# A graph layer with scatter-add: the layer norm without TensorE steps, sorting moved into the loop, early z additions moved

## The chip, the core and the metric

The kernel runs on one core of a Trainium2 chip. The core has five engines that run their own instruction streams and wait for each other through semaphores: TensorE (PE; weight loads are listed as PEld), VectorE (DVE), ScalarE (ACT), GpSimd (POOL) and SyncE (SP). DMAs are issued from the queues of SP, ACT and POOL. Matmul results lie in PSUM, all else on the chip in SBUF. The metric is the device time of one execution in microseconds (us); lower is better.

## The reference

6250 nodes with 64 features, 206,250 edges sorted by their target `dst`:

```python
h = jnp.maximum(_layernorm(x, axis=-1), 0.0)
msg = jax.nn.relu(h[src] + edge_attr)
agg = jax.ops.segment_sum(msg, dst, num_segments=N)
z = h + agg
out = x + jax.nn.relu(z @ W1 + b1) @ W2 + b2
```

For each edge a normalized row is fetched by its source, the edge's own row is added, and the result is summed into the row of its target. A small two-layer network follows.

## The kernel before

Edges come in 268 groups of 768 (128 partitions x 6 columns) and a short last one. The normalized rows are needed in three forms: `h_rows` in DRAM for gathers (POOL's indirect DMAs, one column of 128 rows each, `gather`, L204), `hp` in SBUF as three bf16 parts for fetching rows by TensorE, and `z`, features on partitions and nodes along the free axis, as the start of the sum.

*Two ways to fetch a row.* Half of the columns of a group come by gathers, the other half (a "unit" of three columns) by TensorE. For that the sources of each unit are sorted: `places` works out row and part of each source, the rank steps (`rank_at`, `rank_count`, `rank_of`, `rank_marks`, `rank_holds`, `rank_turn`, `source`) count within each part and write index lists to DRAM for a chunk of six units, 46 chunks in all; `find` and `back` turn these lists into one-hot matrices, and `slots_of` (L500) and `pick` (L516) multiply with them. Between the two, `slots_out` copies PSUM to `picked`.

*The sum.* `messages` makes the messages, `one_hot` the matrix of targets within a window of 32 nodes, `window_sum` (L615) multiplies the two, and `sum_into_z` (L578) adds the window to z at a place read at run time. `hidden`, `result` and `store` do the network for 512 nodes at a time when their rows are complete.

*Order.* The order on each engine is the order of the program's text (a manual schedule), so an instruction that waits holds up all behind it on its engine. The text runs as follows.

1. Loads; constants; `places(0, 2)` (chunks 0 and 1), `rank_at(0)`, `rank_count(0)`.
2. The layer norm in four quarters of 13 and 12 rows per partition (`CUTS`, L797): `ln_head` (sum, mean, subtraction on VectorE, square on ScalarE), `ln_rows` (sum of squares, root on ScalarE, reciprocal, scaling with the ReLU; then the write to `h_rows`), `ln_turn` (transposes on TensorE into one of three PSUM banks, four rows each, and their copies to z on ScalarE). The rank steps of chunk 0 are interleaved.
3. `slots_of_edges` (target of each edge within its group; a matmul spreads each group's base over the partitions), the loads and gathers of groups up to 6 (`enter`), `places(2, NCH)` for all other chunks, and `banks_begin` (four matmuls that prime the two pick banks).
4. The F0 loop (L829) over the first five groups, which are fetched by gathers alone. The first three gather raw rows of x, so that they need not wait for `h_rows`, and are normalized here (`norm_edges`). Into their gaps `fill` puts steps of `ln_parts`, which make hp. The rank steps of chunks 1 and 2 and the zeroing of the tail half of each `ea` buffer (`tails_begin`) lie here too, and one window sum and z addition per step.
5. The first slots and picks, and then 276 times `half(u)`: the loop over units. Each issues at most one group's loads and gathers nine groups ahead; the gathers wait for TensorE ("beats").

PSUM: one bank `rows` shared by all small products, three `half` banks for slots (the window sums have a corner of the first), two pick tiles of two banks each.

The four lines that set the second chunk of work in the layer norm:

```python
        if len(rows) > 1:
            ln_turn(*rows[-2])
        if r == CUTS[1]:
            rank_turn(0)
```

Of the kernel before, what the change touches and what calls it, by code (L numbers as in the profile page):

```python
# [75 lines left out]
BIAS, STEP = 4096, 512  # L76
CHECKS = [NG // 4, NG // 2, 3 * NG // 4, NG - 12]
# [4 lines left out]
def kernel(  # L82
# [80 lines left out]
    nc.vector.tensor_copy(ident_b, ident)  # L163
    ones_b = const.tile([P, P], F16, name="ones_b")
# [19 lines left out]
    nc.scalar.copy(z[D:], zero[D:].to_broadcast([P - D, N + W]))  # L184
# [53 lines left out]
    code = const.tile([P, NCH, CC], F32, name="code")  # L238
    assert PARTS <= S

    def from0_all(n):
        return from0[:, :n].unsqueeze(1).to_broadcast([P, RG, n, H])
# [12 lines left out]
    def places(c0, c1):  # L255
        n = c1 - c0
        row = lnp.tile([P, n, CC], I16, name="row", bufs=1)
        off = lnp.tile([P, n, CC], F32, name="off", bufs=1)
        second = lnp.tile([P, n, CC], I16, name="second", bufs=1)
        third = lnp.tile([P, n, CC], F32, name="third", bufs=1)  # L260
        own = lnp.tile([P, n, CC], F32, name="own", bufs=1)
        m, parts = stretches(src_sb, c0, c1)
        for src, w, gs in parts:
            nc.vector.tensor_copy(own.rearrange("p c s -> p (c s)")
                                  .rearrange("p (e w g j) -> p e w g j", w=2, g=m, j=H)[:, :, w, gs], src)
        nc.vector.tensor_scalar(row, own, 1.0 / RR, 0.5 / RR + 0.5, op0=ALU.mult, op1=ALU.add)
        nc.vector.scalar_tensor_tensor(off, row, float(-RR), own, op0=ALU.mult, op1=ALU.add)
        nc.vector.tensor_scalar(second, off, 1.0 / PARTS, (RR + 0.5) / PARTS - 0.5, op0=ALU.mult, op1=ALU.add)
        nc.vector.scalar_tensor_tensor(node[:, c0:c1], second, float(PP), row, op0=ALU.mult, op1=ALU.add)
        nc.vector.tensor_scalar(third, second, float(BB), quarter[:, 0:1], op0=ALU.is_equal, op1=ALU.mult)  # L270
        nc.vector.scalar_tensor_tensor(off, second, float(-PARTS), off, op0=ALU.mult, op1=ALU.add)
        nc.vector.scalar_tensor_tensor(part[:, c0:c1], off, float(RR), third, op0=ALU.add, op1=ALU.add)
        nc.vector.tensor_scalar(code[:, c0:c1], part[:, c0:c1], float(STEP), float(BIAS), op0=ALU.mult, op1=ALU.add)

    spot_rows = dram.tile([NCH * CC, P], BF16, name="spot_rows")
    ats, counts, marks, holds, ranks, spot_i = {}, {}, {}, {}, {}, {}

    def rank_at(c):
        ats[c] = rank.tile([P, RG, PARTS, H], F16, name="at")
        nc.vector.tensor_tensor(ats[c], over(part[:, c], PARTS), from0_all(PARTS), ALU.is_equal)  # L280

    def rank_count(c):
        ps = psum.tile([P, RG, PARTS, H], F32, name="rows", bufs=1)
        at = ats[c]
        nc.tensor.matmul(ps, upper, at, start=True, stop=False)  # L285
        for d in range(1, H):
            last = nc.tensor.matmul(ps[:, :, :, d:], ones_b, at[:, :, :, :H - d], start=False, stop=(d == H - 1))  # L287
        if c < 3:
            beats.append(last)
        counts[c] = rank.tile([P, RG, PARTS, H], F16, name="before", bufs=1)  # L290
        nc.scalar.copy(counts[c], ps)

    def rank_of(c):
# [7 lines left out]
        nc.vector.tensor_tensor(spot_i[c], ranks[c], code[:, c], ALU.add)  # L301
# [9 lines left out]
    def rank_holds(c):  # L311
        holds[c] = rank.tile([P, RG, S, H], F16, name="holds")
        nc.vector.tensor_tensor(holds[c], over(ranks[c], S), from0_all(S), ALU.is_equal)  # L313
# [9 lines left out]
    def rank_turn(c):  # L323
        turned = psum.tile([CC, P], BF16, name="rows", bufs=1)
        nc.tensor.transpose(turned, spot_i.pop(c).bitcast(BF16), ident_b)  # L325
        sp = rank.tile([CC, P], BF16, name="sp")
# [5 lines left out]
    def source(c):  # L332
# [7 lines left out]
        if c < 2:  # L340
            beats.append(last)
        col = rank.tile([PARTS, RG * S], I16, name="source")
# [7 lines left out]
    halves_made = [0]  # L350

    def next_half():
        halves_made[0] += 1
        return half_banks[halves_made[0] % 3]
# [11 lines left out]
    def ln_rows(r, n, sq):  # L366
        h = x_rows(r, n)
        v = lnp.tile([PP, n], F32, name="ln_v")
        nc.vector.tensor_reduce(v, sq, AX.X, ALU.add)
        nc.scalar.activation(v, v, AF.Sqrt, bias=eps_sb[:PP], scale=1.0 / D)  # L370
        nc.vector.reciprocal(v, v)
# [7 lines left out]

    def ln_turn(r, m, h):  # L380
        zv = z[:D, :NP].rearrange("d (p r) -> d p r", r=RR)
        for i in range(0, m, 4):
            n = min(4, m - i)
            pt = next_half()[:D].rearrange("d (u p) -> d u p", u=4)
            for u in range(n):
                nc.tensor.transpose(pt[:, u, :], h[:, i + u, :], ident[:PP, :PP])  # L386
            nc.scalar.copy(zv[:, :, r + i:r + i + n], pt[:, :n].rearrange("d u p -> d p u"))
# [11 lines left out]
    def combine(xg, ea, n):  # L399
        nc.vector.tensor_tensor(xg[:, :n], xg[:, :n], ea[:, :n], ALU.add)  # L400
        msg = work.tile([P, G, D], F32, name="msg", bufs=3)
# [144 lines left out]
    def norm_edges(xg):  # L546
# [4 lines left out]
        sq = work.tile([P, G, D], F32, name="msg", bufs=3)  # L551
# [11 lines left out]
    pick_banks = [psum.tile([P, H + 1, 4, D], F32, name=f"pick{i}", bufs=1) for i in range(2)]  # L563
# [16 lines left out]
    def one_hot(u):  # L580
        g, (lo, hi) = group_of(u), span(u)
        n = hi - lo
        oh = work.tile([P, G, W], F32, name="oh")
# [9 lines left out]
    def messages(u):  # L593
# [10 lines left out]
        msg = work.tile([P, G, D], F32, name="msg", bufs=3)  # L604
# [91 lines left out]
    def half(u):  # L696
# [60 lines left out]
        chunk(u + 13, rank_count)  # L757
        chunk(u + 12, rank_of)
        chunk(u + 11, rank_marks)
        chunk(u + 11, rank_turn)  # L760
        chunk(u + 10, rank_holds)
        chunk(u + 10, rank_fits)
        chunk(u + 9, source)
        if g in CHECKS and is_first(u):
# [13 lines left out]
    def slots_of_edges():  # L778
# [3 lines left out]
        nc.tensor.matmul(pb[:, :NG + 1], ones[0:1, :], base, start=True, stop=True)  # L782
        nc.vector.scalar_tensor_tensor(
# [8 lines left out]

    heads, rows = [], []
    places(0, 2)
    rank_at(0)
    rank_count(0)
    for r, to in zip(CUTS, CUTS[1:]):  # L797
        heads.append(ln_head(r, to - r))
        if r == 0:
            rank_of(0)  # L800
            rank_marks(0)
            rank_holds(0)
        if len(heads) > 1:
            rows.append(ln_rows(*heads[-2]))
        if len(rows) > 1:
            ln_turn(*rows[-2])
        if r == CUTS[1]:
            rank_turn(0)
            source(0)
    rows.append(ln_rows(*heads[-1]))  # L810
    ln_turn(*rows[-2])
# [7 lines left out]
    slots_of_edges()  # L819
    ln_turn(*rows[-1])  # L820
# [3 lines left out]
    places(2, NCH)  # L824
# [3 lines left out]
    banks_begin()  # L828
    for g in range(F0):  # L829
        for i in range(g * LOOK // F0, (g + 1) * LOOK // F0):  # L830
            tails_begin(i)
# [6 lines left out]
        if g == 1:  # L838
            rank_of(1)
            rank_marks(1)  # L840
            rank_turn(1)
        if g == 2:
            rank_holds(1)
            rank_fits(1)
            source(1)
        if g == 3:
            rank_at(2)
# [7 lines left out]
    sum_into_z(-LAG - 1)  # L855
    while split:
        fill()
    ln_stack.close()
# [16 lines left out]
    for b in range(BB + 1):  # L875
        find(1, b)
    back_far(1)
# [89 lines left out]
```

## Time and profile before

| | us |
|---|---|
| median of 3 runs | 1443.79 |
| lowest, highest | 1442.95, 1453.53 |
| the profiled execution | 1449.7 |
| its span, first to last instruction | 1447.9 |

Busy shares of that span: TensorE 79%, VectorE 67%, ScalarE 66%, GpSimd 56%. The mean granted clock of TensorE was 0.974.

In the views, each line of a timeline gives start and duration in us, engine, line of the code (L...), operation, what is written <- what is read, shapes, count, and in brackets how long the engine had been idle and what released it ("remote" and "another core or an unknown queue" are releases whose origin the profile doesn't have; with one core they are semaphores within it). Groups give busy time, mean ns of one, and the idle time ahead of them. "issue" is waiting that the profile doesn't explain.

### The profile page before, as it was taken

What the parts mean: (1) busy time and instruction counts of PE and PEld (TensorE: products, weight loads), DVE (VectorE), ACT (ScalarE), POOL (GpSimd) and SP (SyncE); (2) the same over time, 40 slices, a digit from 0 to 9 for tenths busy, and PEclk for the clock granted to TensorE, in tenths of its full rate; (3) what the DMA queues carried; (4) which work ended last, traced back from release to release, by engine and by line L of the source; (5) the groups of instructions that cost most, each with busy time, mean ns of one, the idle gap of its engine ahead of it and who ended that gap; (6) DMA issues with size and microseconds to landing.
All of it is one profiled execution on the core that took longest, in us unless ns stands there. A gap on an engine that the chain in (4) does not pass through costs nothing.

```text
span 1447.9 us, 55550 instructions
## 1 busy us (share of the span) xinstructions
PE 1142.2 (79%) x23305; PEld 899.5 (62%) x23305; DVE 977.1 (67%) x2686; ACT 956.8 (66%) x1979; POOL 806.7 (56%) x798
## 2 busy tenths in 40 slices
PE   3158888888788788888888888888888788888887
PEld 2046666666666666666666666666666666666666
DVE  7656666666667677666676667667666666766666
ACT  5356666667667676676676667667666666666666
POOL 5755546565555655555655565555565655556450
PEclk9579999999999999999999999999999999999999
DMA  5333534445444443444444443444444443435341
GB/s 169 90 108 108 150 99 114 130 118 139 109 118 116 139 125 106 124 118 139 109 119 121 129 124 112 124 106 144 116 116 120 134 123 108 134 107 141 114 111 35
DMA packets 115259, 172.40 MB, mean 119 GB/s; under 512 B 28603, under 2 KB 83772, under 8 KB 115004
## 3 DMA queue, kind: packets, MB, share of 16 engines
q1 hardware_dynamic: 89912, 143.05, 32.8%
q0 software_dynamic: 25088, 25.74, 9.1%
q8 instruction: 185, 3.03, 0.9%
q14 instruction: 70, 0.57, 0.1%
q10 hardware_dynamic: 4, 0.01, 0.0%
HBM read 164.86 MB, written 3.84 MB: 117 GB/s over the span
## 4 chain that ended last, share of the span: by engine, by line
PE 77%; issue 17%; DVE 2%; another core or an unknown queue 1%; ACT 1%; POOL 1%; DMA 1%; DVEq 0%; ACTq 0%; POOLq 0%
PE half L500 33%; PE pick L516 31%; PE half L615 9%; PE rows L339 1%; PE rows L287 1%; PE rows L652 1%; POOL xr L204 1%; PE rows L642 1%; PE rows L285 1%; PE rows L325 0%; ACT z L184 0%; DVE hp L397 0%; PE half L386 0%; DVE found L468 0%
## 5 line engine op out<-in xcount | busy, mean ns | idle before, releaser
L204 POOL DMA_INDIRECT xg<-h_rows,src_sb x754 | 772.6, 1025 | 585.0 <-PE half L500 448.5
L500 PE MATMUL half<-hp,found 128*32 128x192 bf16 x14352 | 498.8, 249 | 238.7 <-issue 219.7
L509 ACT CAST picked<-half 128x384 bf16<-128x384 f32 x828 | 369.7, 481 | 395.8 <-remote 222.0
L500 PEld LDWEIGHTS <-found 128*32 128x32 bf16 x14352 | 317.9, 96 | 367.6 <-issue 342.0
L516 PE MATMUL pick<-picked,backs 128*128 128x192 bf16 x4968 | 465.3, 248 | 3.9 <-issue 2.2
L516 PEld LDWEIGHTS <-backs 128*128 128x128 bf16 x4968 | 401.1, 99 | 51.7 <-issue 49.6
L578 DVE TENSOR_TENSOR z<-z,half 128x32 f32 x281 | 52.7, 187 | 380.8 <-issue 174.8
L487 DVE TENSOR_SCALAR backs<-spots,ids 128x768 bf16<-128x768 int16 x690 | 257.9, 416 | 7.5 <-issue 2.0
L603 DVE TENSOR_REDUCE ea<-pick 128x192 f32<-128x576 f32 x276 | 207.9, 753 | 47.9 <-PE pick L516 30.8
L468 DVE TENSOR_SCALAR found<-sources,nodes_of 128x1536 bf16<-128x1536 int16 (+1 forms) x414 | 203.8, 520 | 0.3 <-issue 0.2
L525 ACT COPY pick<-ea 128x576 f32<-128x576 f32 x264 | 168.9, 640 | 0.0
L615 PE MATMUL half<-oh,msg 128*64 128x32 f32 x3224 | 151.1, 227 | 2.7 <-DVE z L578 2.1
L605 ACT ACTIVATE msg<-ea 128x384 f32<-128x384 f32 (+2 forms) x281 | 146.6, 522 | 9.3 <-issue 4.1
L615 PEld LDWEIGHTS half<-oh,msg 128*64 128x64 f32 x3224 | 119.6, 138 | 46.0 <-issue 34.6
L477 ACT ACTIVATE dist<-spots,far 128x768 bf16<-128x768 int16 x138 | 129.9, 942 | 0.0
L480 ACT ACTIVATE backs<-dist,ones 128x768 bf16<-128x768 bf16 x138 | 129.5, 939 | 0.3 <-ACT dist L477 0.3
L584 DVE TENSOR_TENSOR oh<-slot,slots 128x192 f32<-128x192 int16 (+2 forms) x281 | 95.2, 339 | 8.0 <-remote 4.7
L600 DVE TENSOR_TENSOR ea<-ea,xg 128x192 f32<-128x192 f32 x252 | 88.3, 350 | 0.8 <-issue 0.4
L344 ACT CAST source<-rows 24x64 int16<-24x64 f32 x138 | 28.0, 203 | 21.0 <-PE rows L339 11.5
L339 PE MATMUL rows<-holds,marks 128*96 128x96 f16 x276 | 25.8, 231 | 12.7 <-DVE holds L313 8.7
L285 PE MATMUL rows<-at,upper 128*128 128x432 f16 x46 | 16.5, 358 | 21.8 <-issue 11.1
L339 PEld LDWEIGHTS <-marks 128*96 128x96 f16 x276 | 22.9, 147 | 12.9 <-DVE holds L313 8.8
(110 smaller groups left out, 431.1 us busy)
## 6 DMA issues: line engine op xcount, KB each, us to landing
sources<-source_row SPq DMA_DIRECT2D x138, 384.0 KB
ea<-in_edge_attr_dram SPq DMA_DIRECT2D x268, 192.0 KB
spots<-spot_rows SPq DMA_DIRECT2D x138, 192.0 KB
xg<-h_rows,src_sb POOLq DMA_INDIRECT x754
xb<-in_x_dram SPq DMA_DIRECT2D x12, 128.0 KB
out_dram<-o SPq DMA_DIRECT2D x12, 128.0 KB
h_rows<-x SPq DMA_DIRECT2D x3, 384.0 KB
dst_sb<-in_dst_main_dram SPq DMA_DIRECT2D x1, 804.0 KB
```

What stands on the lines that cost most here:

```text
L204: it = nc.gpsimd.indirect_dma_start(out=xg[:, j, :], out_offset=None, in_=rows[:, :], in_offset=bass.IndirectOffsetOnAxis(ap=idx[:, j:j + ...
L468: nc.vector.tensor_scalar(found[k][:, b * PARTS:b * PARTS + n].rearrange("p m i s -> p (m i s)"), sources[k][:, :n * 2 * S], nodes_of[:, b ...
L477: nc.scalar.activation(dists[k], spots[k].bitcast(I16), AF.Abs, bias=far)
L480: nc.scalar.activation(backs[k][:, Q - 1].rearrange("p t s -> p (t s)"), dists.pop(k), AF.Relu, bias=ones[:, 0:1], scale=-1.0)
L487: nc.vector.tensor_scalar(backs[k][:, q].rearrange("p t s -> p (t s)"), spots[k].bitcast(I16), ids[:, q:q + 1], None, op0=ALU.is_equal)
L500: last = nc.tensor.matmul(ps[j * S:(j + 1) * S, u], found[k][:, m, i, :], hp[:, min(m, RR - 1)].rearrange("p t d -> p (t d)"), start=(b == ...
L509: nc.scalar.copy(picked[k][:, n0:n0 + 2], halves.pop((k, n0)))
L516: last = nc.tensor.matmul(ps[:, u, :3].rearrange("p t d -> p (t d)"), backs[k][:, q, i * H + u, :], picked[k][:, i * Q + q], start=False, ...
L525: nc.scalar.copy(picks[u][:, :H, :3], parts)
L603: nc.vector.tensor_reduce(ea[:, c0:c0 + H], picks.pop(u)[:, :H, :3].rearrange("p j t d -> p j d t"), AX.X, ALU.add)
L605: nc.scalar.activation(msg[:, lo:hi], ea[:, lo:hi], AF.Relu)
L615: last = nc.tensor.matmul(pa[i * D:(i + 1) * D], msg[:, j, :], oh[:, j, :], start=(j < lo + 2), stop=(j >= hi - 2))
```

## The change

- **Layer norm.** `ln_rows` is split into `ln_var` (sum of squares and root) and the rest. Two heads are begun, then quarter by quarter. No rank step and no transpose is left in it. `rank_count(0)` and all that follows of chunk 0 come behind, then the zeroing of the lower half of z, which stood at the start on ScalarE; the twelve `tails_begin` stand at the start instead.
- **Transposes.** `ln_turn` only issues the transposes, into the pick banks (four turns of 512 columns), in the steps 0 to 3 of the F0 loop; the copies to z (`ln_turned`) come a step later, in steps 1 to 4. `banks_begin` comes behind the loop.
- **Sorting.** `places` works in 16-bit tiles borrowed from another buffer (`ow`) and gives way after each instruction. Chunks 0 and 1 are done at the start, 2 to 5 behind the layer norm, and the other 40 in three calls (6 to 21, 22 to 37, 38 to 45) in the main loop, one instruction per unit. `code` is gone; `part` holds an offset, and `from_b` is a second iota for it.
- **Handing back.** Each TensorE step with a reader on ScalarE is split in two (`rank_counted`, `rank_turned`, `sourced`), so that the reader can stand later in the text. In the main loop both halves stand next to each other as before.
- **z additions** of the first three groups move behind the first slots. `oh` has four buffers for two, `msg` four for three. `slots_of_edges` has its matmul in `bases`, with `places(2, 6)` between.

```diff
+PLACED = [0, 2, 6, 22, 38, NCH]
...
-    nc.scalar.copy(z[D:], zero[D:].to_broadcast([P - D, N + W]))
...
     def places(c0, c1):
         n = c1 - c0
+        held = [work.tile([P, WB], F32, name="ow").bitcast(I16) for _ in range(2)]
...
         nc.vector.tensor_scalar(row, own, 1.0 / RR, 0.5 / RR + 0.5, op0=ALU.mult, op1=ALU.add)
+        yield
...
-        nc.vector.tensor_scalar(code[:, c0:c1], part[:, c0:c1], float(STEP), float(BIAS), op0=ALU.mult, op1=ALU.add)
...
     pick_banks = [psum.tile([P, H + 1, 4, D], F32, name=f"pick{i}", bufs=1) for i in range(2)]
+    def next_turn():
+        i = turns_made[0] % 4
+        turns_made[0] += 1
+        return pick_banks[i // 2].rearrange("p j t d -> p (j t d)")[:, i % 2 * 512:][:, :512]
...
+    def ln_turned():
+        zv = z[:D, :NP].rearrange("d (p r) -> d p r", r=RR)
+        for pt, r, n in turned_rows:
+            nc.scalar.copy(zv[:, :, r:r + n], pt[:, :n].rearrange("d u p -> d p u"))
+        turned_rows.clear()
...
+        for c, to in zip(PLACED[2:], PLACED[3:]):
+            if u == max(0, 2 * RG * (c // 2) - 60):
+                searches.append(places(c, to))
         if g in CHECKS and is_first(u):
             searches.append(find_left(CHECKS.index(g)))
-        elif searches and next(searches[0], True):
+        if searches and next(searches[0], True):
             searches.pop(0)
...
+    for i in range(LOOK):
+        tails_begin(i)
+    for _ in places(0, 2):
+        pass
     rank_at(0)
+    quarters = list(zip(CUTS, CUTS[1:]))
+    heads = [ln_head(r, to - r) for r, to in quarters[:2]]
+    rows = []
+    for r, to in quarters[2:]:
+        v = ln_var(*heads.pop(0))
+        heads.append(ln_head(r, to - r))
+        rows.append(ln_rows(*v))
+    for v in [ln_var(*heads.pop(0)) for _ in range(2)]:
+        rows.append(ln_rows(*v))
     rank_count(0)
+    rank_counted(0)
+    nc.scalar.copy(z[D:], zero[D:].to_broadcast([P - D, N + W]))
+    rank_of(0)
+    rank_marks(0)
+    rank_turn(0)
+    rank_turned(0)
+    rank_holds(0)
+    source(0)
+    sourced(0)
+    pb = bases()
     split = [ln_parts(*r) for r in rows]
...
+    for _ in places(2, PLACED[2]):
+        pass
+    slots_of_edges(pb)
     rank_fits(0)
     for g in range(F0 + 2):
         enter(g)
-    places(2, NCH)
...
-    banks_begin()
     for g in range(F0):
...
         starts_for(g)
+        if g >= RAW:
+            fill()
...
+        ln_turned()
+        if g < len(rows):
+            ln_turn(*rows[g])
         if g >= 1:
             window_sum(g - 1 - F0)
-        if g > LAG:
-            sum_into_z(g - LAG - 1 - F0)
...
+    rank_counted(2)
+    banks_begin()
...
+    for g in range(F0 - LAG):
+        sum_into_z(g - F0)
     back_far(1)
```

More of the change, by code (lines that the diff above doesn't have):

```diff
@@ L256, in places, with at @@
         n = c1 - c0
[L257 to L261, printed above, removed]
+        held = [work.tile([P, WB], F32, name="ow").bitcast(I16) for _ in range(2)]
+        def at(i):
+            return held[i // 3][:, i % 3 * n * CC:][:, :n * CC].rearrange("p (c s) -> p c s", s=CC)
+        own, off, row, second, third = at(0), at(1), at(3), at(4), at(5).bitcast(F16)
         m, parts = stretches(src_sb, c0, c1)
```

95 lines of the change are left out of this document (49 added, 46 removed).

## The prediction

> **What bounds the kernel now.** I read the page first, then the stages, then the lead-in (everything ahead of the 276 half units) in the timeline. The page's chain line and two of its groups (busy, mean ns | idle before, releaser):
>
> ```profile
> span 1447.9 us, 55550 instructions
> PE 77%; issue 17%; DVE 2%; another core or an unknown queue 1%; ACT 1%; POOL 1%; DMA 1%; DVEq 0%; ACTq 0%; POOLq 0%
> L204 POOL DMA_INDIRECT xg<-h_rows,src_sb x754 | 772.6, 1025 | 585.0 <-PE half L500 448.5
> L578 DVE TENSOR_TENSOR z<-z,half 128x32 f32 x281 | 52.7, 187 | 380.8 <-issue 174.8
> ```
>
> TensorE holds the end for 77% of the span; VectorE and the gathers on POOL have room in the loop. The stages (busy time of PE, PEld, DVE, ACT, POOL, then granted clock, DMA share, GB/s):
>
> ```profile
> 60.00:80.00 20.00, 4.26 (x45) 3.04 (x45) 5.16 (x14) 6.21 (x14) 13.27 (x14) 0.50 0.28 73
> 300.00:600.00 300.00, 247.64 (x5095) 194.90 (x5093) 204.42 (x563) 202.52 (x423) 170.45 (x167) 0.99 0.44 121
> ```
>
> From 300 us on TensorE is busy 83% of the time. In the lead-in no engine is full: at 60 to 80 us TensorE works 4.3 of 20 us, at half the clock, and VectorE 5.2. So the lead-in is made of waits, and the change is nearly all there. Two places hold them. The first is the layer norm (start, duration, idle before and its releaser):
>
> ```profile
> 21.42 1.06 PE L386 MATMUL half<-ident,x 128*64 128x128 f32 x4 [1.10 <-ACT z L387]
> 24.30 1.08 ACT L387 COPY z<-half 64x512 f32<-64x512 f32 x2 [2.94 <-remote]
> 25.00 1.92 PE L386 MATMUL half<-ident,x 128*64 128x128 f32 x8 [2.52 <-ACT z L387]
> 29.25 1.70 ACT L387 COPY z<-half 64x512 f32<-64x512 f32 x3 [3.05 <-remote]
> 29.95 2.77 PE L386 MATMUL half<-ident,x 128*64 128x128 f32 x12 [3.03 <-ACT z L387]
> 31.05 0.65 ACT L387 COPY z<-half 64x512 f32<-64x512 f32 x1
> 31.43 0.96 DVE L372 SCALAR_TENSOR_TENSOR x<-x,ln_v 128x768 f32<-128x768 f32 x1
> 35.62 0.94 POOL L204 DMA_INDIRECT xr<-h_rows,src_sb  x1 [8.39 <-DMA h_rows<-x]
> ```
>
> Four transposes that begin at 29.95 are answered at 31.05, 1.1 us later. The four from 21.42 are answered at 24.30, 2.9 us later, and of the eight from 25.00 the first answer comes at 29.25: TensorE's answers come 1.8 and 3.1 us late. ScalarE stands at these copies, with the next square or root of the layer norm queued behind them, and VectorE stands behind ScalarE. So the last normalized row is made at 32.39, and the first gather from h_rows waits for it until 35.62. The second place is the loop over the F0 = 5 first groups; the chain of waits has there:
>
> ```profile
> 61.95 3.31 issue
> 67.06 4.72 another core or an unknown queue
> 72.52 3.74 another core or an unknown queue
> 77.40 4.69 another core or an unknown queue
> ```
>
> 16.5 us in all. The first of them, with who is asked and who waits:
>
> ```profile
> 56.93 0.86 PE L615 MATMUL half<-oh,msg 128*64 128x32 f32 x12
> 65.26 0.36 DVE L584 TENSOR_TENSOR oh<-slot,slots 128x192 f32<-128x192 int16 x1 [3.31 <-issue]
> ```
>
> The one-hot at 65.26 needs the buffer that the window sum of 56.93 reads (two buffers), so that sum is answered after 8.3 us; the other three waits stand behind later sums in the same way, at a one-hot or at a z addition. The cause of the lateness isn't in the trace. It falls together with gathers in flight: the transposes from 29.95 are prompt, and POOL was idle for the 8.39 us ahead of 35.62.
>
> **The change part by part.** *Layer norm.* The ranks of chunk 0, the transposes and their z copies leave it, and the 5.42 us zeroing of z moves behind it; twelve small zeroings of the ea tails take its place on ScalarE, off the path as the zeroing was. What is left is VectorE's own work, here for the 13-row quarter:
>
> ```profile
> 6.45 1.02 DVE L359 TENSOR_REDUCE ln_s<-x 128x13 f32<-128x832 f32 x1 [0.44 <-DMA x<-in_x_dram]
> 7.51 0.18 DVE L360 TENSOR_SCALAR ln_s<-ln_s 128x13 f32<-128x13 f32 x1
> 7.72 1.02 DVE L361 TENSOR_TENSOR x<-x,ln_s 128x832 f32<-128x832 f32 x1
> 13.18 1.01 DVE L369 TENSOR_REDUCE ln_v<-ln_sq 128x13 f32<-128x832 f32 x1
> 14.56 0.24 DVE L371 RECIPROCAL ln_v<-ln_v 128x13 f32<-128x13 f32 x1 [0.37 <-issue]
> 14.84 1.02 DVE L372 SCALAR_TENSOR_TENSOR x<-x,ln_v 128x832 f32<-128x832 f32 x1
> ```
>
> 4.49 us for 13 rows, so 16.9 for 49. With two heads begun ahead, the squares and roots on ScalarE lie beside VectorE's next quarter; 0.6 us for the turns that stay bare. From 6.45 that ends at 24.0 and not at 32.4. POOL's 18 raw gathers end at 27.2 (35.62 less 8.39), so the first gather from h_rows comes at about 27 and not at 35.62.
>
> *Between layer norm and the F0 loop.* Before:
>
> ```profile
> 9.13 0.38 DVE L295 TENSOR_TENSOR before<-before,at 128x432 f16<-128x432 f16 x1 [0.39 <-ACT before L291]
> 10.65 0.55 DVE L313 TENSOR_TENSOR holds<-rank_of,from 128x576 f16<-128x576 f16 x1
> 3.14 5.42 ACT L184 COPY z<-zero 64x6282 f32<-64x6282 f32 x1
> 14.44 0.24 ACT L327 COPY sp<-rows 18x128 bf16<-18x128 bf16 x1
> 15.40 0.63 ACT L344 CAST source<-rows 24x64 int16<-24x64 f32 x3 [0.73 <-issue]
> 33.01 1.23 PE L782 MATMUL rows<-base,ones 1*128 1x269 f32 x2 [0.29 <-DVE base L780]
> 34.28 1.83 DVE L783 SCALAR_TENSOR_TENSOR slot<-dst_sb,rows 128x1608 int16<-128x1608 int32 x1 [1.42 <-PE rows L782]
> 36.31 0.80 DVE L264 CAST own<-src_sb 128x396 f32<-128x396 int32 x3
> 42.85 0.57 DVE L273 TENSOR_SCALAR code<-part 128x792 f32<-128x792 f16 x1
> ```
>
> places for 44 chunks takes from 36.31 to 43.42, 7.1 us, all of it ahead of the first message; four chunks stay, as ten instructions of 0.2 (the rows of 7.51 and 14.56), 2 us. VectorE alone then needs 2.1 (the ranks' five instructions, 9.13 to 11.20), 0.6 for base (32.39 to 33.01), 2 for places and 2.1 for the slots (1.83 and three short ones), 24.0 + 6.8 = 30.8. But the zeroing of z, put behind the last root, some 2 us ahead of the last row, holds ScalarE until 27.4, and transposition, source lines and the bases follow each other through one PSUM tile: 1.6 us for the two copies with the matmul between (14.44 to 16.03), 1.2 for the bases, so the slots begin at 30.3 and end at 32.4, and the loop begins at about 33. Before, its first instruction stood at 43.34.
>
> *The F0 loop.* VectorE's first instruction in it, and what follows behind it:
>
> ```profile
> 43.34 0.54 DVE L548 TENSOR_REDUCE raw_s<-xr 128x6 f32<-128x384 f32 x1
> 36.73 1.50 PE L570 MATMUL pick<-marks,ones_b 128*128 128x512 f16 x4
> 86.93 4.71 PE L500 MATMUL half<-hp,found 128*32 128x192 bf16 x104 [9.45 <-DVE found L468]
> 93.06 1.65 PE L516 MATMUL pick<-picked,backs 128*128 128x192 bf16 x18 [1.43 <-ACT pick L525]
> ```
>
> The three steps with raw rows take from 43.34 to the first of the four waits at 61.95, 18.6 us, and keep that: 33 + 18.6 = 51.6. The z additions and the buffer wait of the one-hots go (four buffers each; additions behind the slots), so 61.95 to 82.1 goes but for what the moved transposes put there. The first two quarters lie beside VectorE's long steps. The third and fourth don't, since steps 3 and 4 are short: 2.77 of transposes and three copies of 0.65 each, 2 x 4.7 = 9.4, with the last parts of hp beside them. The four priming matmuls of the pick banks, 1.5, now wait for the last copy, since the transposes use those banks. Then slots to first pick, 6.1, as at 86.93 to 93.06: 51.6 + 9.4 + 1.5 + 6.1 = 68.6, 24.5 us ahead of 93.06.
>
> *Late answers* are the unknown. Four handoffs from TensorE stand bare: the bases (33.01 to 34.28, prompt, no gather then; now gathers run), the third and fourth quarter, and the fourth quarter's start, queued behind a window sum. Lower end 0 (nothing can come early), upper end 4.7 each, the window sums' usual wait. I take 2 each, between the transposes' own 1.8 and 3.1 and the prompt ones: 8 us. **Net 16.5 us.**
>
> *The main loop.* 40 chunks of places go there, one instruction per half unit, 30 in all; by 7.1 us for 44 chunks they are at least 6.5 us, and by fixed parts about 10. VectorE idles 380.8/281 = 1.36 us ahead of each z addition, which covers one instruction of 0.3; if that cover were gone it would cost 10 us. I take 0. The cheaper code, iota and buffer edits cost nothing that is on the path.
>
> One row speaks against putting places under gathers:
>
> ```profile
> 39.87 1.32 POOL L204 DMA_INDIRECT xr<-h_rows,src_sb  x1 [0.30 <-issue]
> ```
>
> It ran beside places; the gather at 35.62, ahead of it, took 0.94. The Trainium skill, SBUF — State Buffer, "SBUF: two separate sides", says that GpSimd can't write a gather's descriptors while VectorE runs an operation in a mode that takes the port they share. By that rule the trace agrees, and 30 gathers in the loop would grow by 0.4, 12 us on POOL. POOL stands 448.5 us waiting for TensorE in the loop, so it isn't on the path, and the sum keeps its value either way.
>
> **The rivals.** *Late answers eat most of it*: 4.7 for each bare handoff, and 1.2 each for two half-covered ones (the second quarter, a msg buffer; about 3.5 us of VectorE work over them), 21 us, so a gain of about 3: 1440. For it: all four window sums are late; against it: half of the transposes are prompt. *Slower*: the same place, with the lateness of 56.93 to 65.26, 8.3 us: 4 x 8.3 + 2 x 4.8 = 43 against 24.5, 18 us slower, 1462. It turns to a loss above 5.3 us each; only one of the six late answers seen is so late. *Gathers decide*: POOL begins only 9 us earlier, so if the first units had to wait for it the gain would be 9: 1435. Against it: groups are entered 9 ahead, and POOL waits for TensorE.
>
> **How the numbers follow.** The profiled execution took 1449.7 (span 1447.9), 0.4% over the median of 1443.79; the 16.5 us are lead-in and come off either: 1433.2 there, 1427 as a median. Chances: forecast 0.60 (gains of 11 to 24.5), late answers 0.24, gathers 0.08, slower 0.08. Range: from all of 24.5, 1419, to the late-answer case, 1442; about 2 in 10 stay outside. About 1%, 14.4 us, is what can be told from no change: gains above it are most of the forecast, 0.56; within, 0.37; slower 0.07.
>
> **What would show it.** Last h_rows write issued at 24 and not 32.4; first raw_s near 33; no wait over 1 us at one-hots or z additions; first pick between 67 and 78; half units of the same length after. Wrong if ScalarE stands 4 us or more at the z copies of the third and fourth quarter, if the bases come after 35, or if units with a places instruction are longer than their neighbours.

## The result, and the profile after

The change makes no difference. The median after is 1450.19 us (14 runs, 1446.62 to 1453.16), the median before 1450.67 (14 runs, 1442.95 to 1456.8); after over before is 1.0002, 95% interval 0.9984 to 1.002. The forecast was 1427. Some 7 us of that distance are the base it was taken from, a median of three runs, 1443.79; the rest is a gain of 16.5 us that isn't there.

In some sets of runs (taken on one chip, one after the other) a half unit of the loop takes about 5.0 us and the kernel before 1427 to 1451, as above, in others about 3.5 and 1055 to 1056, with the changed kernel always on the same side; these are called long and short runs here.

The timeline of the changed kernel in its lead-in:

```profile
22.43 0.96 DVE L400 SCALAR_TENSOR_TENSOR x<-x,ln_v 128x768 f32<-128x768 f32 x1
28.55 0.95 POOL L207 DMA_INDIRECT xr<-h_rows,src_sb  x1 [0.30 <-issue]
32.52 0.55 DVE L583 TENSOR_REDUCE raw_s<-xr 128x6 f32<-128x384 f32 x1
49.47 0.55 DVE L583 TENSOR_REDUCE raw_s<-xr 128x6 f32<-128x384 f32 x1
55.48 0.22 DVE L584 TENSOR_SCALAR raw_s<-raw_s 128x6 f32<-128x6 f32 x1 [5.46 <-remote]
61.78 0.91 ACT L421 COPY z<-pick 64x512 f32<-64x512 f32 x2 [10.11 <-remote]
63.04 0.55 DVE L590 TENSOR_REDUCE raw_v<-msg 128x6 f32<-128x384 f32 x1 [4.73 <-ACT msg L587]
64.87 0.95 POOL L207 DMA_INDIRECT xg<-h_rows,src_sb  x1 [7.17 <-PE half L649]
86.51 0.48 ACT L544 CAST picked<-half 128x384 bf16<-128x384 f32 x1 [3.94 <-remote]
87.58 3.04 PE L551 MATMUL pick<-picked,backs 128*128 128x192 bf16 x18 [7.71 <-issue]
```

The first three lines are near the forecast: the last normalized row ends at 23.39, the first gather from `h_rows` starts at 28.55, the F0 loop at 32.52. Then things stand still. The line at 55.48 is the plainest: VectorE takes the mean of a sum that it has made itself in the instruction ahead (49.47), no other engine has a part in it, and it starts 5.46 us late. ScalarE stands for 10.11 us ahead of its copies of z at 61.78, and POOL, whose next gather waits for a window sum, stands for 7.17. The first pick comes at 87.58, 5.5 us ahead of the 93.06 of before; without the stops it would be near 68.

The loop, in the groups of the page (busy, mean ns | idle before, releaser), and its stages:

```profile
L207 POOL DMA_INDIRECT xg<-h_rows,src_sb x754 | 776.8, 1030 | 588.2 <-PE half L535 446.4
L612 DVE TENSOR_TENSOR z<-z,half 128x32 f32 x281 | 52.9, 188 | 369.1 <-issue 177.9
```

```profile
60.00:85.00 25.00, 12.42 (x193) 9.25 (x194) 13.85 (x32) 15.75 (x32) 12.94 (x12) 1.00 0.37 111
300.00:600.00 300.00, 248.41 (x5114) 195.57 (x5102) 206.80 (x574) 202.94 (x425) 171.65 (x168) 0.99 0.42 121
```

Busy times in the groups and in the stage from 300 to 600 are those of before within 1.2%. One of the three groups of places instructions lies in that stage, and the half units 71 to 83, which hold it, average 4.92 us in both kernels. So the places in the loop cost nothing that shows here, and the loop is as long as it was.

Where the 5.5 us went is seen from the gathers. Their starts, out of the two traces:

| gather | before, us | after, us |
|---|---|---|
| 19th, first from `h_rows` | 35.6 | 28.6 |
| 81st | 138.4 | 135.0 |
| 401st | 715.0 | 711.2 |
| last, 784th | 1408.8 | 1408.0 |

From the 19th to the 81st, 62 gathers, they take 1.66 us each before and 1.72 after; in a half unit with three gathers, 5.04 us in both, 1.68. The lead-in and the loop look like one stream of gathers at one pace, and the changed kernel starts it 7.1 us earlier and gives up half of that by the 81st.

### The profile page after: what moved, and what is told of

It reads as the page before. It is cut to its first block, busy times and chain, and to the rows that moved or that the text cites. A ratio compares the mean times of both kernels' runs of the same rounds, so it can differ in the third digit from the quotient of the medians.

```text
span 1448.1 us, 55574 instructions
## 1 busy us (share of the span) xinstructions
PE 1144.0 (79%) x23305; PEld 901.4 (62%) x23305; DVE 977.9 (68%) x2714; ACT 955.8 (66%) x1979; POOL 810.8 (56%) x799
## 5 line engine op out<-in xcount | busy, mean ns | idle before, releaser
L207 POOL DMA_INDIRECT xg<-h_rows,src_sb x754 | 776.8, 1030 | 588.2 <-PE half L535 446.4
L535 PE MATMUL half<-hp,found 128*32 128x192 bf16 x14352 | 497.4, 248 | 225.2 <-issue 215.4
L339 PE MATMUL rows<-ident_b,spot_i 128*18 128x128 bf16 x46 | 10.4, 226 | 24.9 <-DVE rank_of L312 17.3
L312 DVE TENSOR_REDUCE rank_of<-before 128x18 f16<-128x432 f16 x46 | 27.7, 603 | 2.2 <-issue 0.7
```

The source lines that it names most:

```text
L207: it = nc.gpsimd.indirect_dma_start(out=xg[:, j, :], out_offset=None, in_=rows[:, :], in_offset=bass.IndirectOffsetOnAxis(ap=idx[:, j:j + ...
L535: last = nc.tensor.matmul(ps[j * S:(j + 1) * S, u], found[k][:, m, i, :], hp[:, min(m, RR - 1)].rearrange("p t d -> p (t d)"), start=(b == ...
```

## The experiments

Two theories stood against each other at first. G: gathers that POOL issues back to back hold up the signals (semaphore updates) of all engines. P: TensorE's answers are late by themselves. A third, B, blamed the bytes that are moved.

### Gathers taken away, paced; transposes left out (short runs)

*lead_plain*: in `load`, the 36 gathers from `h_rows` ahead of the loop become plain DMAs.

```diff
+        if RAW <= g < 14:
+            nc.sync.dma_start(out=xg[:, lo:hi], in_=h_rows[:(hi - lo) * P].rearrange("(j p) d -> p j d", p=P))
+            return ea, xg
         gather(xg[:, lo:], src_sb[:, g * G + lo:g * G + hi], hi - lo, x if g < RAW else h_rows, behind)
```

> The changed kernel with its 36 gathers from h_rows ahead of the loop of half units (groups 3 to 13) put as plain DMAs of the same rows per partition and the same bytes on SP's queue, one per group; it fetches fixed rows in place of those named by src. Theory G (gathers issued back to back by POOL hold up the signals of all engines): the long waits between 38 and 90 us go, the first pick starts at 68 to 73 us and not at 87.6, and the profiled time falls by 14 to 19 from 1449.9, to 1431 to 1436, with half units unchanged at 5.04 us. Rival P (TensorE's answers are late by themselves, at half clock and with fp32 transposes): waits and first pick stay, 85 to 90. Rival B (the bytes moved hold things up): the same, 85 to 90.

*lead_paced*: in `gather`, behind each of these 36.

```diff
+            if lead[0] and rows is not x:
+                nc.gpsimd.iota(pad, pattern=[[1, PAD]], base=0, channel_multiplier=0,
+                               allow_small_or_imprecise_dtypes=True)
```

> The changed kernel with an iota of about 0.5 us on POOL behind each gather from h_rows ahead of the loop, so that gathers start every 1.8 us and not every 1.25. Theory G, with a shared path that needs 1.4 to 1.6 us per gather: the path keeps up, waits over 3 us in the F0 loop go, first pick at 69 to 76 us. If the number of gathers counts and not their pace, the waits spread and the first pick stays at 83 to 90. Rival P: first pick 85 to 90. The whole time: 1435 to 1450 by theory G, since the gathers of the loop must still be made; 1450 by the rivals.

*no_turns*: in the F0 loop, with z zeroed whole.

```diff
-        ln_turned()
-        if g < len(rows):
-            ln_turn(*rows[g])
```

> The changed kernel without the 49 transposes of h and their 13 copies to z in the F0 loop; z is zeroed whole and so lacks h. Theory G: gathers still run from 28 to 58 us and other handoffs are late in the place of these, first pick at 78 to 88. Rival P: nothing of the lateness is left, first pick at 60 to 70.

*all_plain*: the edit of lead_plain with `if g >= RAW`.

> The changed kernel with all gathers from h_rows, 766, put as plain DMAs of the same bytes on SP's queue, one per group, with no pacing behind TensorE; it fetches fixed rows. Theory G: the loop's half units are set by gathers too; without them they take 3.3 to 3.6 us and not 5.04, and the whole takes 1000 to 1080 us. Rival P (TensorE is the bound at 83% busy): half units of at least 4.2, 1230 us or more. Rival B (bytes): half units of 5.0, 1430 to 1450.

All four were short runs, where the kernel before took 1056.16: lead_plain 1047.15, lead_paced 1067.19, no_turns 1060.73, all_plain 1052.41 (one run each), with first picks at 66.0, 65.4, 62.7 and 66.7. Nothing was late in any of them, so they tell nothing of G, P and B. One number stands out: lead_paced. Its groups on POOL:

```profile
L210 POOL DMA_INDIRECT xg<-h_rows,src_sb x754 | 774.0, 1026 | 226.3 <-issue 95.7 <-PE half L541 51.4 <-DMA xg<-h_rows,src_sb 28.7
L216 POOL IOTA pad<- 128x112 f32 x36 | 9.7, 268 | 0.3
```

The iotas took 0.27 us each, about half of what had been expected. The idle time, 226.3 us, is 0.30 for each of 754 gathers: POOL never stopped. And 9.7 us of iotas in the lead-in put the end of this one run off by 9.8 against the changed kernel's 1057.39 in the next set.

### The two kernels in short runs

> The changed kernel itself, on whatever chip this falls to, since the kernel before took 1056.2 us on the chip of lead_plain, no_turns and all_plain, and 1450.7 on that of the first measurements. Theory G, widened: how long a gather holds up the signals of the engines differs from chip to chip, and the change acts on what is left. Where gathers take 1.6 us each out of a half unit of 5.04, first pick at 87.6, about 1450 and no difference from before. Where they don't (half units near 3.5), no wait over 2 us in the F0 loop, first pick at 62 to 67, and then either faster by about 10 us (places in the loop are covered) or the same within 3 (half units with a places instruction are longer, since TensorE and VectorE are at 94% and 92%).

> The kernel before, for its trace on the same chip. Theory G: where half units are near 3.5 us, the four waits at window sums (16.5 us in the first trace) are gone and its first pick comes at 74 to 79 and not at 93. Rival P, lateness is TensorE's own: the waits are there on any chip, first pick at 90 to 95.

The changed kernel took 1057.39, the kernel before 1055.38: 1.0011, 0.999 to 1.0033. So no difference here either, but by another way. First picks and POOL, after_again first, before_again second:

```profile
28.33 0.95 POOL L207 DMA_INDIRECT xr<-h_rows,src_sb  x1 [0.30 <-issue]
32.30 0.55 DVE L583 TENSOR_REDUCE raw_s<-xr 128x6 f32<-128x384 f32 x1
46.18 0.54 DVE L583 TENSOR_REDUCE raw_s<-xr 128x6 f32<-128x384 f32 x1
46.76 0.21 DVE L584 TENSOR_SCALAR raw_s<-raw_s 128x6 f32<-128x6 f32 x1
66.45 1.65 PE L551 MATMUL pick<-picked,backs 128*128 128x192 bf16 x18 [1.21 <-ACT pick L560]
```

```profile
31.32 0.95 POOL L204 DMA_INDIRECT xr<-h_rows,src_sb  x1 [4.04 <-DMA w_sb<-in_w_dram]
74.27 1.65 PE L516 MATMUL pick<-picked,backs 128*128 128x192 bf16 x18 [1.12 <-ACT pick L525]
```

VectorE's mean at 46.76 follows its sum by 0.04 us, where it came 5.46 late in the long run. The first pick at 66.45 is the forecast's sum without its late answers, 68.6, within 2.2. Before, it stands at 74.27 and not at 93.06: the same program runs without the four waits of 16.5 us behind window sums, so they are no fixed cost of TensorE's steps. The changed kernel is 7.8 us ahead at the first pick and at nothing at the end. POOL's groups say why, again after_again first:

```profile
L207 POOL DMA_INDIRECT xg<-h_rows,src_sb x754 | 769.1, 1020 | 229.9 <-issue 93.9 <-PE half L535 54.3 <-DMA xg<-h_rows,src_sb 27.7
L207 POOL DMA_INDIRECT xr<-in_x_dram,src_sb x18 | 19.1, 1059 | 5.4 <-issue 5.4
L207 POOL DMA_INDIRECT xr<-h_rows,src_sb x12 | 12.0, 1002 | 3.7 <-issue 3.7
```

```profile
L204 POOL DMA_INDIRECT xg<-h_rows,src_sb x754 | 764.7, 1014 | 229.9 <-issue 93.9 <-PE half L500 45.8 <-DMA xg<-h_rows,src_sb 34.2
L204 POOL DMA_INDIRECT xr<-in_x_dram,src_sb x18 | 18.5, 1030 | 5.4 <-issue 5.4
L204 POOL DMA_INDIRECT xr<-h_rows,src_sb x12 | 14.1, 1174 | 7.4 <-DMA w_sb<-in_w_dram 4.0 <-issue 3.4
```

Busy and idle added to the first gather's start (3.8 and 3.6) give 1043.0 and 1043.6, and the last gathers end at 1042.6 and 1043.4. POOL issues gathers without a pause from the start to the end; in the changed kernel only the one pause of 4.0 us is gone, and its gathers are longer by 4.4 in all. Call this theory S: the stream of gathers sets the end, and what comes ahead of it counts only where it moves the stream. The rival L has it that lead-in and loop add up, and the loop got longer.

### S against L (short runs)

> The kernel of lead_plain once more, timed beside before_lead_plain on one chip. Where half units are near 3.5 us: theory S (the stream of gathers, which POOL issues back to back from 4 to 1042 us, sets the end, so that what comes ahead of it counts for nothing) gives 1045 to 1050, some 8 us less than before_lead_plain, since here POOL begins its stream at the first units. Where half units are 5.04 (the first chip): theory G gives a first pick at 66 to 72 and 1430 to 1440; rivals P and B 85 to 90 and 1450.

*before_lead_plain* is the edit of lead_plain in the kernel before.

> The kernel before with the same 36 gathers put as plain DMAs of fixed rows. Where half units are near 3.5 us: theory S gives a first pick at 74, as in before_again, and a time 6 to 10 us above lead_plain_3, 1053 to 1058: the lead-in that the change saves then shows. Rival L (the loop of the changed kernel is longer by what the lead-in gained, places included): the same time as lead_plain_3 within 3 us. On the first chip: theory G gives a first pick at 72 to 78 and not at 93, and 1430 to 1440.

*places_left_out*:

```diff
-        for c, to in zip(PLACED[2:], PLACED[3:]):
-            if u == max(0, 2 * RG * (c // 2) - 60):
-                searches.append(places(c, to))
...
+    for t in (part, node):
+        nc.vector.tensor_copy(t[:, PLACED[2]:], t[:, 5:6].to_broadcast([P, NCH - PLACED[2], CC]))
```

> The changed kernel without the 30 instructions of places in the loop: part and node of chunks 6 to 45 are copies of chunk 5 (two instructions ahead of the loop), so other rows are summed. Rival L: half units of the stretch are shorter, 8 to 10 us less than the changed kernel, 1047 to 1050 where half units are near 3.5. Theory S: gathers beside VectorE get a little shorter, at most 4 us less, 1053 to 1058. On the first chip both give 1445 to 1451.

lead_plain_3 took 1043.2 (0.9894 of the kernel before, 0.9867 to 0.992), a little under the expected range, before_lead_plain 1053.04 (0.9974, 0.9952 to 0.9997). With the stream beginning only at the first units, the saved lead-in is worth 9.8 us by the medians, as S has it and L not. The two recorded runs lie only 2.9 us apart (1048.34 and 1051.28). Their gathers, lead_plain_3 first:

```profile
L207 POOL DMA_INDIRECT xg<-h_rows,src_sb x730 | 743.6, 1019 | 260.0 <-PE half L538 88.0 <-issue 87.8 <-DMA xg<-h_rows,src_sb 29.0
```

```profile
L204 POOL DMA_INDIRECT xg<-h_rows,src_sb x730 | 737.9, 1011 | 269.3 <-PE half L503 98.8 <-issue 88.8 <-DMA xg<-h_rows,src_sb 24.4
```

The stream of lead_plain_3 has 9.3 us less idle time and 5.7 us more of gathers, and its last gather ends 2.7 earlier. That the end goes with the stream is seen here too; the 9.8 us are not seen in this pair. places_left_out took 1049.68 (0.9957, 0.9933 to 0.998), with its number inside what L expected. Its gathers:

```profile
L207 POOL DMA_INDIRECT xg<-h_rows,src_sb x754 | 761.0, 1009 | 229.9 <-issue 94.5 <-PE half L535 49.7 <-DMA xg<-h_rows,src_sb 28.0
```

They take 8.1 us less than in after_again, the whole 7.7 less (5.7 by the ratios to the kernel before, as the two are of different sets), and POOL still never pauses (3.8 us, busy 792.0 and idle 239.0 give 1034.8, the last gather ends at 1034.5). So the end goes with the stream, as S has it, but by more than the 4 us that S allowed. And it isn't shown how places lengthen the stream. In after_again 31 gathers run beside one of the 30 places instructions; they take 1054 ns on average, the other 723 take 1019, which makes 1.1 us in all (2.0 in after_third). Set against the same gathers of places_left_out, they hold 1.3 of the 8.1 us. The same loop also differs between runs by some 5 us, 774.0 in lead_paced and 769.1 in after_again. Nor are the half units with a places instruction longer, as L has it: those from 71 to 83 average 3.43 us in after_again, 3.39 in places_left_out.

### Two more (long runs)

*places_ahead* does all of `places(6, 46)` ahead of the F0 loop.

```diff
+    for c, to in zip(PLACED[2:], PLACED[3:]):
+        for _ in places(c, to):
+            pass
     for g in range(F0):
         messages(g - F0)
```

> The changed kernel with its places for chunks 6 to 45 all done ahead of the F0 loop, and none in the loop of half units. VectorE's 24 instructions there put the first pick off by 6 to 10 us, to 72 to 77 where half units are near 3.5. Theory S (POOL's unbroken stream of gathers sets the end): the first pick doesn't count, the stream starts and runs as in the changed kernel and its gathers are shorter without places beside them, so 1047 to 1052, 4 to 8 us under the kernel before. Rival L (lead-in and loop add up): 1055 to 1060. On the first chip (half units of 5.04), theory G: 1445 to 1452, no difference from before.

*more_whole*:

```diff
-HEAD, PERIOD = 2 * RG - 1, 4 * RG - 1
+HEAD, PERIOD = 2 * RG - 1, 2 * RG - 1
-WHOLE = [F0 + RG - 1] + list(range(F0 + HEAD + 2 * RG - 1, NG + 1, PERIOD))
+WHOLE = [F0 + RG - 1] + list(range(F0 + HEAD + RG - 1, NG + 1, PERIOD))
...
-        n, g0 = (HEAD, F0) if c0 == 0 else (PERIOD, F0 + HEAD + (c0 - 2) // 4 * PERIOD)
+        n, g0 = (HEAD, F0) if c0 == 0 else (PERIOD, F0 + HEAD + (c0 - 2) // 2 * PERIOD)
```

> The changed kernel with every eleventh group, and not every twenty-third, fetched wholly by TensorE: 288 half units for 276, 36 gathers fewer. Where half units are near 3.5, TensorE takes over as the bound: 288 half units of about 3.4 us behind a first pick at 66, and 15 us of end, 1055 to 1065, and POOL now waits for TensorE. On the first chip, theory G (some 1.6 us per gather bound the loop): 36 gathers fewer are 50 to 60 us less against 12 half units of little more than their share, 1390 to 1420; rival P (TensorE is the bound there): 12 half units more at 4.9, about 1500.

The kernel before took 1426.8. places_ahead took 1434.93 (1.0055, 1.0039 to 1.007), where I expected no difference. Its gathers in the lead-in:

```profile
52.60 0.95 POOL L207 DMA_INDIRECT xg<-h_rows,src_sb  x1 [0.30 <-issue]
60.62 1.54 POOL L207 DMA_INDIRECT xg<-h_rows,src_sb  x1 [7.08 <-PE rows L298]
70.43 1.28 POOL L207 DMA_INDIRECT xg<-h_rows,src_sb  x1 [5.65 <-PE half L649]
78.42 0.95 POOL L207 DMA_INDIRECT xg<-h_rows,src_sb  x1 [3.37 <-PE half L649]
```

The gathers of groups 7 and later wait for matmuls of the F0 loop, and with that loop put off the stream has gaps of 7.1, 5.7 and 3.4 us. Its first pick comes at 96.2, and its 81st gather starts at 142.4, 7.4 later than in the changed kernel of the first set. That fits a stream, but I had overlooked that it can be interrupted there.

more_whole took 1435.93 (1.0061, 1.0038 to 1.0084), outside of what either theory gave. Half units with three gathers took 4.96 us, with one 3.54, with none 3.31, but those with two 4.72. Had the stream alone bound the loop, 36 gathers fewer would have shown; that two gathers cost nearly as much as three was not followed up. So no fixed price of a gather gives the length of the long loop.

### Gathers taken away again (long runs)

> The kernel of lead_plain (36 gathers ahead of the loop as plain DMAs), in the hope of a chip with half units of about 5 us. There: theory G gives no wait over 3 us between 38 and 70 us, first pick at 66 to 72 and not at 88, and a time 10 to 20 us under the kernel before of the same chip; rivals P and B give a first pick at 85 to 90 and no difference. On a chip with half units near 3.5: as before, first pick at 66, 10 to 12 us under the kernel before.

> The kernel of all_plain (all 766 gathers from h_rows as plain DMAs of the same bytes). On a chip with half units of about 5 us: theory G2 (TensorE's work of some 3.2 us per half unit, and 0.6 us of held signals for each gather on top) gives half units of 3.3 to 3.6 and 1040 to 1080 us; rival B (any DMA of these bytes holds signals up) 4.8 to 5.1 and 1400 to 1450. On another chip 1048 to 1056.

> The kernel of lead_paced (an iota of 0.27 us behind each of 36 gathers, so 1.54 us between starts ahead of the loop). On a chip with half units of about 5 us: if a gather holds a shared path for 1.4 us, the backlog no longer grows and the first pick comes at 70 to 80; if a gather costs its hold whatever the pace, 84 to 92. On another chip 9 to 11 us over the changed kernel, 1065 to 1069, as POOL's stream sets the end there.

The kernel before took 1428.24 in this set (one run each). all_plain_s took 1046.67: 766 gathers replaced by DMAs of the same bytes are worth 381.6 us, and half units fall to 3.51. So it is neither the bytes nor TensorE's own work. (These DMAs also read fixed rows, come from SP's queue and don't wait for TensorE, so the runs don't tell which property of a gather it is.) TensorE's slots in the changed kernel of the first set, and in all_plain_s:

```profile
L535 PE MATMUL half<-hp,found 128*32 128x192 bf16 x14352 | 497.4, 248 | 225.2 <-issue 215.4
```

```profile
L538 PE MATMUL half<-hp,found 128*32 128x192 bf16 x14352 | 351.2, 247 | 5.4 <-issue 4.6
```

The 225 us in which TensorE waits for nothing that the profile shows go with the gathers, and so do 146 us of its "busy" time for the same 14352 matmuls. lead_plain_s took 1397.32, 30.9 less, more than the 10 to 20 of theory G, and from its timeline:

```profile
64.20 1.16 POOL L207 DMA_INDIRECT xg<-h_rows,src_sb  x1 [35.82 <-PE half L538]
67.39 1.65 PE L554 MATMUL pick<-picked,backs 128*128 128x192 bf16 x18 [1.58 <-ACT pick L563]
```

With no gathers from `h_rows` ahead of it, but with all the transposes and copies, the first pick comes at 67.39: rival P falls, and the forecast's sum without late answers, 68.6, holds in a long run too.

lead_paced_s took 1420.13, with the first pick at 85.55, which spoke for number and against pace. But its F0 loop ran through without a late signal until 62 us; then TensorE's slots came in bursts:

```profile
78.23 0.36 PE L541 MATMUL half<-hp,found 128*32 128x192 bf16 x4 [0.40 <-issue]
79.65 0.38 PE L541 MATMUL half<-hp,found 128*32 128x192 bf16 x4 [1.06 <-issue]
81.07 0.38 PE L541 MATMUL half<-hp,found 128*32 128x192 bf16 x4 [1.04 <-issue]
```

Four matmuls each 1.42 us, while a gather starts each 1.37 us. These matmuls belong to one line and wait for nothing that the profile shows ("issue"). So it isn't only the answers from one engine to another that are late, as G has it, but also the starts of an engine's own next instructions. A wider pace was tried next, with PAD at 512 and not 112.

### Pace

> The changed kernel once more, to stand beside lead_paced_2 in one call. Where half units take about 5 us: first pick at 87 to 89 and the same time as the kernel before within 0.5% (it gains 5 us at the first pick). Where they take 3.5: first pick at 66 to 67, the same time as before within 0.5%.

> The changed kernel with a longer iota behind each of the 36 gathers from h_rows ahead of the loop, about 0.8 us, so some 2.0 us between starts. Where half units take about 5 us: if pace matters (a gather holds a shared path for about 1.4 us), nothing is late and the first pick comes at 67 to 75; if the number counts, 84 to 92 as in lead_paced_s (85.6). Where they take 3.5: theory S, 28 to 32 us over the changed kernel, the iotas' own time.

These two were short runs: after_third 1058.11 against 1055.1 (1.0026, 1.0005 to 1.0046), lead_paced_2 1083.48, 25.4 more (28 to 32 expected), of which its iotas are 23.2. In the next set it was a long one:

> The kernel of lead_paced_2 again. Where half units take about 5 us: if pace matters, nothing is late ahead of the first pick, which comes at 67 to 75; if the number counts, 84 to 92. Where they take 3.5: 1080 to 1087, as in lead_paced_2.

It took 1450.51, the kernel before 1449.44 (one run each). Its timeline:

```profile
68.28 2.06 PE L557 MATMUL pick<-picked,backs 128*128 128x192 bf16 x15 [2.48 <-ACT pick L566]
84.49 1.66 PE L557 MATMUL pick<-picked,backs 128*128 128x192 bf16 x18
88.52 1.65 PE L557 MATMUL pick<-picked,backs 128*128 128x192 bf16 x18 [0.27 <-ACT pick L566]
91.90 1.66 PE L557 MATMUL pick<-picked,backs 128*128 128x192 bf16 x18
93.79 0.96 POOL L210 DMA_INDIRECT xg<-h_rows,src_sb  x1 [0.16 <-issue]
95.54 0.96 POOL L210 DMA_INDIRECT xg<-h_rows,src_sb  x1 [0.16 <-PE half L541]
96.80 1.00 POOL L210 DMA_INDIRECT xg<-h_rows,src_sb  x1 [0.30 <-issue]
98.11 0.94 POOL L210 DMA_INDIRECT xg<-h_rows,src_sb  x1 [0.30 <-issue]
99.36 1.04 POOL L210 DMA_INDIRECT xg<-h_rows,src_sb  x1 [0.30 <-issue]
125.56 0.86 ACT L550 CAST picked<-half 128x384 bf16<-128x384 f32 x2 [25.98 <-remote]
126.07 2.26 PE L557 MATMUL pick<-picked,backs 128*128 128x192 bf16 x13
```

And its stages (busy time of PE, PEld, DVE, ACT, POOL, then clock, DMA share, GB/s):

```profile
60.00:96.00 36.00, 31.41 (x717) 26.37 (x716) 34.91 (x79) 28.81 (x59) 32.76 (x39) 0.95 0.49 133
96.00:126.00 30.00, 9.52 (x74) 4.28 (x71) 5.07 (x15) 2.77 (x7) 19.89 (x22) 0.62 0.17 38
```

With 1.70 us or more between the starts of gathers nothing is late. The first pick comes at 68.28, and half units follow each other at 3.4 to 4.8 us. At 96.80 the iotas are over, POOL issues a gather each 1.25 us, and two or three us later nearly all stops: ScalarE waits 25.98 us for slots, TensorE does 74 matmuls in 30 us where it did 717 in 36. The DMA engines are not full then, 17% busy at 38 GB/s. So in this run the lateness comes with the pace of the gathers. And nothing of the earlier first pick is left: the 81st gather starts at 134.7, against 135.0 in the changed kernel without iotas. A lead of 19.3 us at the first pick was paid back in eight half units.

## Why the prediction was wrong

- **Layer norm, from 32.4 to 24.0: right.** 23.39. So are the first gather (about 27; 28.55), the slots' start (30.3; 30.32), the F0 loop's (about 33; 32.52) and the sum to the first pick without late answers (68.6; 67.39, 68.28 and 66.45 in the runs in which nothing was late).
- **Late answers, four by 2 us, 8 in all: the first step that failed.** They were 19.0 (87.58 less 68.6), against an upper end of 4.7 for each, 18.8. And they weren't bound to handoffs from TensorE: VectorE stood 5.46 us for its own sum. I had the clue on record, that lateness "falls together with gathers in flight", and still priced it by the handoffs that I could count. The gathers ran under the F0 loop in both kernels; in the changed one VectorE's 5.46 us ahead of 55.48 lie inside the steps with raw rows, which the sum took over as 18.6 us without a late answer.
- **"The 16.5 us are lead-in and come off either": the second step.** Even the 5.5 us that were gained at the first pick didn't come off the end, and 24.8 of lead_paced_2s didn't either. In the first long runs and lead_paced_2s the 81st gather starts at 134.7 to 138.4 with first picks from 68.28 to 93.06; in a short run POOL's stream has no gap from 3.8 to 1042.6 us. What the change moves is that stream: 7.1 us at its start and 0.8 at its end in the first traces, 3.0 and 0.8 in the short ones. In the short runs this is shown by the stream itself; for the long loop it is shown that the gathers make it long (all_plain_s), not by what rule, since more_whole goes against a fixed pace. Where 36 gathers fell away and the lateness with them (lead_plain_s), 30.9 us did come off the end.
- **The rival "gathers decide" came nearest to the mechanism, with a chance of 0.08.** Its gain of 9 us wasn't there either. I argued against it that POOL stands 448.5 us waiting for TensorE. Those are waits that the program sets to pace its gathers, and TensorE, for which they wait, stands itself behind held signals (225.2 us of idle at the slots, 5.4 without gathers). TensorE's 77% of the chain was no proof of a bound: with the gathers replaced, the run with the same matmuls took 381.6 us less. The rival "late answers eat most of it" (0.24) had the size at the first pick, a gain of 3 against 5.5, by luck: its price for each handoff isn't where the time went. "Slower" (0.08) needed more than 24.5 us of lateness in all.
- **Places in the loop at nothing: right in the measured runs**, where the stages from 300 to 600 us are equal. In short runs leaving them out took 5.7 to 7.7 us off (places_left_out), with shorter gathers on POOL; the ceiling of 10 held, and POOL, which I called "not on the path", was the path. The rule cited from the Trainium skill, SBUF — State Buffer, "SBUF: two separate sides", is that GpSimd can't write a gather's descriptors while VectorE holds the port they share. These runs don't bear out the 12 us that were worked out with it from one row: the 30 or 31 gathers beside a places instruction are longer than the others by 1.1 us in all in after_again, 2.0 in after_third and 2.2 in the first trace after the change, and most of the 8.1 us of places_left_out lies in gathers that had none beside them.

What stays open: which part of the chip a gather occupies, why long and short runs differ, why two gathers in a half unit cost nearly what three do, and whether the recording of the runs has a part in the lateness. A pace of the gathers through the whole loop wasn't tried, and no version was found that beats both kernels in both kinds of runs.

## What to carry to other kernels

Before a lead-in is shortened, find what runs through it and into the loop without being done earlier, here, in the short runs, a fixed number of gathers at a fixed pace, and ask when its last one ends; only what moves that is gained. An engine that waits for another can still be the bound, if the other stands behind what the first one does: take its work away in an experiment before the busy shares are believed. And when a wait's cause is unknown but coincides with something, let the estimate follow what it coincides with, and not the places where it was seen.

## What the runs showed of the hardware

- In long runs, with gathers issued each 1.25 us, all engines stand: VectorE 5.46 us for its own earlier instruction, ScalarE up to 25.98 us, and TensorE in front of matmuls that wait for nothing that the profile shows. POOL's time for a gather is nearly the same as in short runs (1030 and 1020 ns on average), and plain DMAs of the same bytes hold up nothing. Whether signals or the starts of instructions are held isn't told apart.
- Ahead of the loop nothing was late at 1.70 us or more between the starts of gathers; at 1.37 some was, and lead_paced_s was prompt for 32 us at 1.52 on average. An estimate from these puts the limit between 1.4 and 1.7 us per gather. It doesn't carry over to the loop, where two gathers in a half unit of 4.72 us (2.36 for each) cost nearly what three did.
- While engines are held, TensorE works in bursts of some matmuls, in lead_paced_s up to four each 1.42 us.
- The 18 gathers of raw rows during the layer norm, at 1.38 us each (after), held up nothing.
- In long runs the traces hold fewer semaphore updates: 11,564 in that of the changed kernel, 26,773 in after_again. This goes with the gathers as well: without them there are 19,656 in a set of long runs (all_plain_s) and 20,062 in a set of short ones (all_plain). Every run here was recorded, so whether the recording has a part in the lateness was not tried.
- In short runs the same program takes 1057 us and not 1450. The traces don't show what differs; chip number 10 showed both kinds.
